# A block's down projection by seven products of half-size blocks in place of eight

## The chip, the cores and the metric

The kernel runs on one core of a Trainium2 chip. A core has five engines with instruction queues of their own, which run side by side and wait for each other through semaphores: TensorE (PE in the profile; its weight loads, PEld, overlap its matmuls), VectorE (DVE), ScalarE (ACT), GpSimd (POOL) and SyncE (SP, which here only starts transfers). SBUF is the on-chip memory of 128 partitions, PSUM the accumulator memory that TensorE writes and that VectorE and ScalarE read. The metric is the device time of one execution in microseconds, as the median of several.

## What is computed

The reference is a gated cross-attention followed by a gated feed-forward layer, for 8 sequences ("blocks") of 256 tokens with 1024 features. The change is in the second half:

```python
def qlinear(x, w):                       # fake_quant: s = max|t| / 127, q = round(t / s) * s
    xq = fake_quant(x, axis=-1)          # one step s for each token
    wq = fake_quant(w, axis=1)           # one step s for each output feature
    return jnp.einsum('bsh,oh->bso', xq, wq)
gate = qlinear(x, w_gate)                # 1024 -> 2752
up = qlinear(x, w_up)
h = jax.nn.silu(gate) * up
return qlinear(h, w_down)                # 2752 -> 1024, the "down" product
```

The result is multiplied by `tanh(g_ffn)` and added to the layer's input, the residual. The kernel keeps the rounded values as whole numbers of at most 127 in bf16 and applies the steps after the products.

## The kernel before

**Stages.** Up to about 457 us the kernel multiplies the two attention weights, runs attention for seven blocks and prepares the feed-forward weights: the down weights end as whole numbers in `wd`, 22 chunks of 128 rows by 1024 columns. Then comes the head, in which the last block's attention lies between the first block's gate and up products; then seven rounds of one block each; then a tail.

**Gate and up, `gate_up`.** A block's 2752 hidden features are 22 chunks, taken as 11 pairs. For each pair TensorE makes 64 passes of 128x256 (`products`, L787, the last pair 48) into one PSUM bank of tag g and one of tag tr. Two banks of each tag exist, so TensorE can be at most two pairs ahead. VectorE multiplies the gate by the token steps (L797, reads ps_g), ScalarE applies silu (L799), VectorE multiplies by the up value (L812, reads ps_tr), ScalarE takes absolute values (L818), and VectorE folds them into a running maximum (`fold`, L829, two SBUF inputs). The last pair has one half chunk, for which L812 reads ps_g as well.

**A round, for b = 1 to 7.** It runs the gate and up products of block b and then the down product of block b-1, while block b is being rounded. `block_max` (L845, L849) and `block_scales` (L857 to L865) turn the maximum into a row of inverse steps, `ib`. `quantised` multiplies each pair by `ib` on VectorE (L876, two SBUF inputs) and rounds it, on VectorE in one instruction (L878) or on ScalarE in two (L880, L881), into `hq`, bf16 of 128 x 2 x 256.

**The down product.** A block's output is two token halves t by two column halves of 512. `down_pair` (L890) makes, for each of the 11 pairs, two passes of 128x512 for each of these four quarters: 88 passes a block, into two banks each of the tags s and a. In the next round `down_end` finishes one quarter after each of the first gate and up pairs: VectorE reads the bank and multiplies by both steps (L907), GpSimd adds the residual (L910), which SyncE has loaded (L899), and GpSimd's queue starts the store (L911).

**The tail.** Block 7 has no products beside it: three quarters one after another, the fourth in two halves, the last addition on VectorE (L1040), the last store on SyncE.

**Order.** In the head all engines run in the order of the program. From the second block on, only TensorE's and VectorE's order is written by hand; the instructions of ScalarE, GpSimd and SyncE are placed by a scheduler.

## Time and profile before

| | us |
|---|---|
| median of 3 runs (932.33 to 933.81) | 932.4 |
| the profiled execution, whole | 931.42 |
| its span, first to last instruction | 929.6 |
| TensorE busy in the span | 923.5 (99%) |
| VectorE / ScalarE / GpSimd busy | 635.6 / 420.9 / 152.0 |
| the head, 457.0 to 506.7: VectorE, GpSimd busy | 31.9, 2.7 of 49.7 |
| the second block's gate and up, 506.7 to 544.7: VectorE, GpSimd busy | 29.2, 0.8 of 38.0 |
| a down product in the steady state, 601.7 to 621.1: VectorE, GpSimd busy | 11.7, 0.0 of 19.4 |
| gate and up in the steady state, 564.1 to 601.7: VectorE, GpSimd busy | 25.9, 7.6 of 37.6 |
| the tail, 906.0 to 929.6: TensorE, GpSimd busy | 19.3, 12.8 of 23.6 |

A line of the page or of its groups names a source line, an engine and an operation, then what it writes and reads with the shapes and the number of instructions, then the busy time in all, the mean of one in ns, and the idle time of the engine before it with what ended it. A line of the timeline has the start and the length in us first. The length of an instruction starts when it is issued, so it includes time in which it is held up; instructions of one engine overlap by about 0.08 us, so that a VectorE instruction of "0.69" follows the one before it after 0.61.

### The profile page before, as it was taken

How to read it: one execution, taken by the hardware profiler on the slowest of the kernel's cores; microseconds unless marked ns; L12 is line 12 of the kernel's file. 1: busy time of each engine (PE TensorE's matmuls, PEld its weight loads, DVE VectorE, ACT ScalarE, POOL GpSimd, SP SyncE). 2: the span in 40 equal slices, each digit the busy share in tenths (PEclk: the TensorE clock that was granted, in tenths of full speed). 3: DMA queues.
4: the chain of work that ended last, by engine and by line, in shares of the span. 5: the costliest groups of instructions: out<-in, count | busy, mean ns of one | idle time of the engine just before them, and what ended most of it. 6: DMA issues, size and time to landing. Idle time of an engine off the chain costs nothing.

```text
span 929.6 us, 14411 instructions
## 1 busy us (share of the span) xinstructions
PE 923.5 (99%) x5471; PEld 689.3 (74%) x5471; DVE 635.6 (68%) x1284; ACT 420.9 (45%) x720; POOL 152.0 (16%) x165
## 2 busy tenths in 40 slices
PE   9999999999999999999999999999999999999998
PEld 5444687878787878787878867858688685876854
DVE  5978845868686767776367778666576665757663
ACT  0123434454545445453547776444354544535440
POOL 0034211212121212132001003012030110302005
PEclk9999999999999999999999999999999999999999
DMA  9359977989888888997979985929669395782704
GB/s 334 119 156 316 297 185 235 230 248 241 247 246 252 238 252 227 247 242 241 235 265 320 321 295 200 344 79 385 204 244 336 84 377 172 280 299 94 303 1 159
DMA packets 139189, 221.96 MB, mean 239 GB/s; under 512 B 92056, under 2 KB 93360, under 8 KB 128880
## 3 DMA queue, kind: packets, MB, share of 16 engines
q1 hardware_dynamic: 129328, 196.12, 68.1%
q0 software_dynamic: 5040, 17.06, 4.7%
q10 hardware_dynamic: 4752, 7.87, 2.4%
q8 instruction: 43, 0.70, 0.3%
q14 instruction: 26, 0.21, 0.1%
HBM read 167.52 MB, written 32.26 MB: 215 GB/s over the span
## 4 chain that ended last, share of the span: by engine, by line
PE 94%; DMA 3%; DVE 1%; POOL 1%; SPq 0%; issue 0%; ACT 0%; POOLq 0%; DVEq 0%; ACTq 0%
PE ps_g L787 17%; PE ps_tr L787 16%; PE ps_g L548 15%; PE ps_s L548 9%; PE ps_a L890 7%; PE ps_s L890 7%; PE ps_s L566 6%; PE ps_a L595 6%; PE ps_tr L445 3%; PE ps_s L342 2%; PE ps_a L342 2%; PE ps_tr L342 1%; PE ps_g L342 1%; DMA raw<-in_L_ffn_w_gate_dram 1%; DMA w_dram<-wt 1%; POOL o L910 1%
## 5 line engine op out<-in xcount | busy, mean ns | idle before, releaser
L787 PEld LDWEIGHTS <-wp 128*128 128x128 bf16 x2752 | 269.3, 98 | 33.0 <-issue 0.3
L787 PE MATMUL ps_g<-xqb,wp 128*128 128x256 bf16 x1408 | 168.1, 273 | 0.0
L787 PE MATMUL ps_tr<-xqb,wp 128*128 128x256 bf16 x1344 | 161.1, 273 | 0.0
L548 PE MATMUL ps_g<-xT,mt 128*128 128x256 f32 x640 | 144.6, 379 | 0.2 <-ACT xT L468 0.2
L548 PEld LDWEIGHTS ps_g<-xT,mt 128*128 128x128 f32 x640 | 120.3, 190 | 19.1 <-issue 3.3
L890 PEld LDWEIGHTS <-hq 128*128 128x128 bf16 x726 | 71.1, 98 | 76.5
L799 ACT ACTIVATE g<-g,swg 128x256 f32<-128x256 f32 (+1 forms) x176 | 80.3, 499 | 59.4 <-DVE g L797 59.4
L812 DVE SCALAR_TENSOR_TENSOR h<-ps_tr,swu,g 128x256 f32<-128x256 f32 x168 | 74.0, 480 | 48.3 <-PE ps_tr L787 34.1
L220 POOL TENSOR_SCALAR raw<-raw,inv 128x1024 f32<-128x1024 f32 (+1 forms) x44 | 56.2, 1276 | 249.1 <-DVE inv L122 144.0
L910 POOL TENSOR_TENSOR o<-o,xr 128x512 f32<-128x512 f32 x31 | 39.2, 1265 | 309.5 <-DVE o L907 287.5
L797 DVE TENSOR_TENSOR g<-ps_g,sx 128x512 f32<-128x512 f32 x88 | 60.7, 690 | 40.0 <-PE ps_g L787 36.9
L548 PE MATMUL ps_s<-xT,mt 128*128 128x256 f32 x384 | 86.9, 379 | 0.0
L818 ACT ACTIVATE g<-h 128x512 f32<-128x512 f32 (+2 forms) x88 | 52.0, 591 | 72.8 <-DVE h L812 72.0
L890 PE MATMUL ps_a<-wd,hq 128*128 128x512 bf16 (+1 forms) x352 | 84.0, 366 | 0.0
L890 PE MATMUL ps_s<-wd,hq 128*128 128x512 bf16 x330 | 84.0, 379 | 0.0
L257 ACT ACTIVATE rq<-raw,nmagic 128x1024 bf16<-128x1024 f32 (+1 forms) x44 | 50.6, 1150 | 62.1 <-POOL raw L220 51.4
L548 PEld LDWEIGHTS ps_s<-xT,mt 128*128 128x128 f32 x384 | 71.2, 190 | 8.7
L876 DVE TENSOR_TENSOR h<-h,ib 128x512 f32<-128x512 f32 x88 | 57.3, 685 | 21.2 <-ACT ib L865 21.2
L829 DVE TENSOR_TENSOR acc<-acc,g 128x512 f32<-128x512 f32 (+2 forms) x88 | 61.6, 700 | 1.0
L566 PE MATMUL ps_s<-fT,H 128*128 128x256 f32 x256 | 58.9, 379 | 0.0
L595 PE MATMUL ps_a<-fn,pT 128*128 128x512 f32 x128 | 57.6, 592 | 0.0
L126 DVE TENSOR_REDUCE wam<-raw 128x1 f32<-128x1024 f32 (+1 forms) x44 | 53.3, 1212 | 5.2 <-DMA raw<-in_L_ffn_w_gate_dram 5.1
(169 smaller groups left out, 1001.5 us busy)
## 6 DMA issues: line engine op xcount, KB each, us to landing
wp<-w_dram SPq DMA_DIRECT2D x80, 1024.0 KB, 6.8
w_dram<-wt SPq DMA_DIRECT2D x43, 256.0 KB, 4.1
raw<-in_L_ffn_w_gate_dram SPq DMA_DIRECT2D x21, 512.0 KB, 5.2
raw<-in_L_ffn_w_up_dram SPq DMA_DIRECT2D x21, 512.0 KB, 4.7
fn<-in_ctx_dram SPq DMA_DIRECT2D x8, 1024.0 KB, 6.7
raw<-in_L_ffn_w_down_dram SPq DMA_DIRECT2D x16, 512.0 KB, 6.7
xr<-in_x_dram SPq DMA_DIRECT2D x16, 512.0 KB, 4.2
x_dram<-xr POOLq DMA_DIRECT2D x16, 512.0 KB, 4.6
```

The lines of the kernel that those rows point to most:

```text
L220: nc.gpsimd.tensor_scalar(raw[:n], raw[:n], inv, MAGIC, ALU.mult, ALU.add)
L342: nc.tensor.matmul(pm, lhsT=a[:, c, k * P : (k + 1) * P], rhs=b[:, c, :], start=start, stop=stop)
L548: nc.tensor.matmul(ph, lhsT=mt[:, k, j * P : (j + 1) * P], rhs=xT[:, k, :], start=(k == 0), stop=(k == KC - 1),)
L566: nc.tensor.matmul(ps[:, :L], lhsT=H[:, j, t * P : (t + 1) * P], rhs=fT[:, j, :], start=(j == 0), stop=(j == KC - 1),)
L595: nc.tensor.matmul(pas[h], lhsT=pT[:, l, :], rhs=f_tiles[b][:, l, halves[h]], start=(l == 0), stop=(l == NLT - 1),)
L787: nc.tensor.matmul(banks[slot // 2][:, slot % 2, :], lhsT=w[:, slot, k, :], rhs=block["xq"][:, k, :], start=(k == 0), stop=(k == KC - 1),)
L797: nc.vector.tensor_tensor(g, pg, block["sx"].to_broadcast((P, 2, TB)), ALU.mult)
L799: nc.scalar.activation(g[:n, i, :], g[:n, i, :], AF.Silu, scale=swg[:n, c : c + 1])
L812: nc.vector.scalar_tensor_tensor(h[:n, i, :], src, swu[:n, c : c + 1], g[:n, i, :], ALU.mult, ALU.mult)
L829: nc.vector.tensor_tensor(acc[:n, i, :], acc[:n, i, :], g[:n, i, :], ALU.max)
L876: nc.vector.tensor_tensor(h, h, ib.to_broadcast((P, 2, TB)), ALU.mult)
L890: nc.tensor.matmul(pds[t, half][:, cols], lhsT=hq[p][:, i, t * P : (t + 1) * P], rhs=wd[:, c, half * HB + cols.start : half * HB + cols.stop],
```

## The change

The down product of a block is a product of two 2x2 block matrices for each pair of chunks: even and odd chunk by two token halves, even and odd chunk by two column halves. The new kernel makes seven products in place of eight (`down_product`, m = 1 to 7), of sums and differences of the quarters. Sums of two whole numbers of at most 127 are exact in bf16.

- **Weights, once.** `weight_sums(p)` makes for each of the 11 pairs a difference of 128x1024 and a sum of 128x512 on VectorE, and a sum of 128x1024 on GpSimd, which overwrites parts of `wd`. They are in the head: pairs 0 to 2 between the two softmax halves, 3 to 6 ahead of the first gate and up pair, 7 to 10 after its pairs 3, 7, 8 and 9.
- **Hidden values, for each block.** `hidden_sums` makes 640 columns of sums for each pair in three instructions (256, 128, 256), on GpSimd during the gate and up products, in the tail on VectorE.
- **Outputs.** m3 and m4 are copied out of PSUM by ScalarE (`evicted`), then eight additions or subtractions on VectorE (`combined_down`) put the four quarters together. `down_end` scales a quarter by the token steps on ScalarE, and multiplies by the column steps and adds the residual on GpSimd. The residual's load moves from SyncE's to GpSimd's queue.
- **Order.** `block_max` comes after 15 passes of the down product (before: 32), `block_scales` after 27 (before: 48). Eight pairs are rounded during the down product and the last three during the next gate and up products.
- **First and last.** In the second block's gate and up products, and for block 7, four of the 11 multiplications by `ib` go to GpSimd. In the tail a share of the last two quarters is prepared ahead (`tail_share`, one on VectorE, one on GpSimd) and `tail_end` adds the last product to it.

```diff
-    def down_pair(pds, hq, p, keys, cols=slice(0, HB)):
-        for t, half in keys:
-            for i, c, n in parts_of(p):
-                nc.tensor.matmul(
-                    pds[t, half][:, cols], lhsT=hq[p][:, i, t * P : (t + 1) * P],
...
+    def weight_sums(p):
+        even, odd = wd[:, 2 * p, :], wd[:, 2 * p + 1, :]
+        nc.vector.tensor_tensor(wdiff[:, p, :], odd, even, ALU.subtract)
+        nc.vector.tensor_tensor(wsum[:, p, :], even[:, :HB], odd[:, HB:], ALU.add)
+        o = 2 * p * D + HB
+        nc.gpsimd.tensor_tensor(
+            wd_flat[:, o : o + D].rearrange("p (i d) -> p i d", i=2),
+            wd[:, 2 * p : 2 * p + 2, :HB], wd[:, 2 * p : 2 * p + 2, HB:], ALU.add,
+        )
+    def hidden_sums(gs, p, hq, parts=(0, 1, 2), engine=nc.gpsimd):
...
+            engine.tensor_tensor(g[:, 0:2, :], v[:, 0], v[:, 1], ALU.add)
+            engine.tensor_tensor(g[:, 2, :], v[:, 0, 0], v[:, 1, 1], ALU.add)
+            engine.tensor_tensor(g[:, 3:5, :], v[:, :, 1], v[:, :, 0], ALU.subtract)
+    def down_product(m, hq, gs, tag, cols=slice(0, HB), pairs=range(NPR), pm=None):
...
+                1: lambda: (gs[p][:, 2, :], wsum[:, p, lo]),
+                2: lambda: (gs[p][:, 1, :], even[:, lo]),
+                3: lambda: (hq[p][:, 0, :P], wdiff[:, p, hi]),
+                4: lambda: (hq[p][:, 1, P:], wdiff[:, p, lo]),
+                5: lambda: (gs[p][:, 0, :], odd[:, hi]),
+                6: lambda: (gs[p][:, 3, :], even[:, hi]),
+                7: lambda: (gs[p][:, 4, :], odd[:, lo]),
+    def down_end(b, t, half, c, sh, xr=None, queue=nc.gpsimd):
...
+        nc.scalar.activation(c, c, AF.Identity, scale=sh[:, t : t + 1])
+        nc.gpsimd.tensor_tensor(c, c, swd_bc[:, cols], ALU.mult)
+        nc.gpsimd.tensor_tensor(c, c, xr, ALU.add)
+        queue.dma_start(out=out[b, t * P : (t + 1) * P, cols], in_=c)
...
     for p in range(2, NPR):
-        hq.append(quantised(first["h"][p - 2], ib, p - 2, nc.scalar))
+        if p < 9:
+            hq[p - 2] = quantised(first["h"][p - 2], ib, nc.scalar)
...
+        if 2 < p < 7:
+            stepped(first["h"][p + 4], ib, nc.gpsimd)
+        if p > 6:
+            hq[p] = rounded(first["h"][p])
...
+            hidden_sums(gs, q, hq[q])
         gate_up(second, p, banks if p == 2 else None)
...
+        m3 = down_product(3, hq, gs, "s")
+        c3 = evicted(m3, "c3")
+        m4 = down_product(4, hq, gs, "a", pairs=range(4))
+        am = block_max(block, "g")
+        down_product(4, hq, gs, "a", pairs=range(4, NPR), pm=m4)
+        c4 = evicted(m4, "c4")
+        m2 = down_product(2, hq, gs, "s", pairs=range(5))
+        next_sh, ib = block_scales(b, am, "tr")
...
+        quantise(0, 1)
+        c21 = combined_down(sum_tile("c21"), m2, c4)
+        m5 = down_product(5, hq, gs, "a")
+        quantise(2, 3)
+        c12 = combined_down(sum_tile("c12"), m5, c3, ALU.subtract)
+        combined_down(c3, m2, c3)
+        combined_down(c4, c4, m5, ALU.subtract)
+        m1 = down_product(1, hq, gs, "s")
+        quantise(4)
...
+    for end, xr in zip(ends, xrs + [xr_tail[b - 1, 1, 1], xr_tail[b - 1, 0, 0]]):
+        down_end(*end, xr)
+    for p in range(NPR):
+        hidden_sums(gs, p, hq[p], (0,), nc.vector)
...
+    down_end(b, 1, 0, b21, sh, xr_tail[b, 1, 0], nc.sync)
...
+    down_end(b, 0, 1, b12, sh, xr_tail[b, 0, 1], nc.sync)
...
+    tail_share(1, 1, b3, sh, xr_tail[b, 1, 1], nc.vector)
+    tail_share(0, 0, b4, sh, xr_tail[b, 0, 0], nc.gpsimd)
...
+    for i in range(2):
         cols = slice(i * HB // 2, (i + 1) * HB // 2)
...
+        m7 = down_product(7, hq, gs, "s", cols)
+        tail_end(0, 0, m7, nsh, b4, cols)
```

## The prediction

> **What bounds the kernel now.** I read the page's busy table and its chain of waits first, then the groups, then the timeline of four places: a down product, a fold beside GpSimd, the head, the end.

> ```profile
> PE 923.5 (99%) x5471; PEld 689.3 (74%) x5471; DVE 635.6 (68%) x1284; ACT 420.9 (45%) x720; POOL 152.0 (16%) x165
> ...
> PE 94%; DMA 3%; DVE 1%; POOL 1%; SPq 0%; issue 0%; ACT 0%; POOLq 0%; DVEq 0%; ACTq 0%
> ```

> TensorE works throughout at the full granted clock (the page's PEclk row is 9 in all slices), and the list of TensorE's waits holds under 2 us. So a pass removed is time gained, as long as nothing else begins to hold TensorE. GpSimd is at 16%: the change fills it. The timeline of TensorE in a steady down product gives the price of a pass:

> ```profile
> 557.25 1.03 PE L890 MATMUL ps_s<-wd,hq 128*128 128x512 bf16 x4
> 558.11 1.03 PE L890 MATMUL ps_a<-wd,hq 128*128 128x512 bf16 x4
> ```

> Four passes start every 0.863 us: 0.216 us each (the "379 ns" of the groups is the length of one, mostly overlapped). The second thing to see is what VectorE and GpSimd do to each other, with and without company:

> ```profile
> 687.00 1.26 POOL L910 TENSOR_TENSOR o<-o,xr 128x512 f32<-128x512 f32 x1 [1.38 <-DVE o L907]
> 687.05 0.69 DVE L797 TENSOR_TENSOR g<-ps_g,sx 128x512 f32<-128x512 f32 x1
> 687.66 1.15 DVE L829 TENSOR_TENSOR acc<-acc,g 128x512 f32<-128x512 f32 x1
> ...
> 694.65 0.68 DVE L829 TENSOR_TENSOR acc<-acc,g 128x512 f32<-128x512 f32 x1
> ```
> ```profile
> 76.99 0.69 DVE L347 TENSOR_TENSOR A<-A,A 128x512 f32<-128x512 f32 x1
> 77.16 2.03 POOL L220 TENSOR_SCALAR raw<-raw,inv 128x1024 f32<-128x1024 f32 x1 [1.49 <-DVE inv L122]
> 77.59 0.68 DVE L347 TENSOR_TENSOR B<-B,B 128x512 f32<-128x512 f32 x1
> ...
> 103.75 1.12 POOL L220 TENSOR_SCALAR raw<-raw,inv 128x1024 f32<-128x1024 f32 x1 [1.95 <-DVE inv L122]
> ```

> The fold has two SBUF inputs and takes 1.15 instead of 0.68 beside GpSimd: it ends 0.55 after GpSimd's 688.26. L797, with one input in PSUM, is not touched. The other way, GpSimd's 1.12 became 2.03 behind two VectorE instructions back to back: it got in only after both.

> [...] Read alone, the first row could be a surcharge of 0.47 for each meeting. [...]

> **Prices.** VectorE, start to start: 0.61 for 512 f32 elements (L876, two in 1.29), about 1.0 ns an element and 0.1 fixed. No bf16 instruction with two SBUF inputs is in the trace. [...] GpSimd: 1.265 for 512 with two inputs (L910); its one-input rows, 1111 ns at 1024 and 843 at 704, show 0.25 fixed. So about 2.3 for 1024 and 1.9 for a pair's 256, 128 and 256; with 0.1 fixed (its smallest memset) 2.4 and 1.75. bf16 on GpSimd is not shown either. A store or load issued there costs 0.56, and 0.3 more between sum and store.

> **Part 1, the passes.** 77 for 88, eleven fewer: 2.37 us a block. Seven rounds: **-16.6**. Block 7 is counted in part 5.

> **Part 2, the head.** VectorE gets 11 x 0.95, GpSimd 11 x 2.3. VectorE is idle ahead of 458.4, but the sums stand behind the first softmax scale. Six instructions back to back, 459.3 to 462.2; GpSimd then takes its first sum to 464.7; eight more VectorE instructions end at 468.5. The first gate (L797) stood at 463.8: 4.7 late. ScalarE, in program order, turns the second probabilities late behind the first |h|, and the second attention product starts at 473.3 instead of 472.5. By pair 7, L812 ends at about 505.3 instead of 500.8. From there a pair costs VectorE: sums 0.95, start of GpSimd's sum 0.1, its 2.3 (the next L797 runs inside it), fold 0.6, L812 0.8 = 4.75, against TensorE's 3.49. Three such pairs: pair 10's L812 ends at 519.7. It reads the half chunk from a g bank that TensorE needs for the next group but one, which began at 510.2: **+9.5**. Bounds: +3 if the exclusion doesn't bind, +12 with 1.1 for 1024. Ahead of the end of the head GpSimd also holds the residual's stores behind seven sums (x2 from 470.1 to about 483.5); landing 4.6 later, 488.1, it is just in time for ScalarE's y0 at 489.

> **Part 3, the first hidden sums.** GpSimd starts when `ib` is there (518.2 before): four multiplications 5.1, 11 x 1.9 = 20.9, and it stands aside for 9 folds, 7 multiplications and 4 roundings of VectorE, 11.0. That is 37.0 after `ib`; m2's last pair is due at 544.7 + 7.3, that is 33.8 after it: **+3.2** (0 to 7).

> **Part 4, a steady round**, 54.6 us long, T from the first down pass. GpSimd: 8 x 1.265 for the outputs, 20.9, 8 transfers 4.5, gaps 1.2, memset 0.3: 37.0. Its first output is ready at T+9.95 (m2 ends at 7.7, two multiplications and a rounding, the sum, ScalarE's scale). It stands aside for 9 multiplications, 3 roundings, 10 folds: 12.5. So it is done at 59.4, T+4.8 of the next down product; m2's last pair is due at T+7.3. Spare 2.5: **0**, and a loss if a pair costs over 2.1. Everything else fits. `block_max` comes 3.24 after the first pass, and the folds end at 2.95 (604.66 against 601.71). The second transposes come 2.81 behind it, and ScalarE's input takes 2.36 (608.62 to 610.98). VectorE: 37.6 busy, plus 8 x 0.61, minus 4 x 0.74 for L907, is 39.5 of 54.6. ScalarE: 26.8, plus two copies, four scalings, one rounding more (about 5.4), is 32 of 54.6. SyncE loses four loads; its weight loads don't move. Two banks of each tag let VectorE be about 4 us late in gate and up, and waits for GpSimd of some 0.5 a fold stay inside that.

> **Part 5, the last down product and the tail.** From T+6.9 GpSimd has 18 instructions in a fixed order: 4 multiplications, 8 for block 6, 6 for block 7. The last of them is the share of the last quarter, for which `tail_end` waits. 18 x 1.265 = 22.8. VectorE's excluded work in the same stretch: 7 multiplications 4.2, 7 roundings 2.5, 33 hidden sums 6.1, the other share 1.2: 14.0. One at a time they need 36.8, so the share can't be there before T+43.7, that is 26.6 after the tail's start (T+17.05); walked in order, with the hidden sums back to back ahead of GpSimd, 28.9. I take 27.5. Then addition, product, addition 1.3, and 3.2 to the end as now (926.44 to 929.6): 32.0. TensorE is done long before, at 16.8. Before, 906.05 to 929.6 is 23.55: **+8.5**. The bounds: without exclusion GpSimd ends at 16, TensorE is last again and the tail is 2.4 shorter; +10 by the walk, +13 with one bf16 element a cycle.

> **Sum** on the profiled execution's 931.4: -16.6 + 9.5 + 3.2 + 0 + 8.5 = +4.6, so 936.0. The median before is 1.0 above that execution; I predict **936.5**.

> **Rivals.** (a) *The exclusion is only paid in the tail*, where both engines are full; in the head and the second block VectorE's spare time takes it: -16.6 + 3 + 8.5 = -5.1, **926**. For it: VectorE was busy 31.9 of 49.7 in the head; against it: part of that idle time is the wait for silu, which stays. (b) **Faster on one mechanism: meetings cost a surcharge of 0.47, or GpSimd slips in between VectorE's instructions.** Then a pair in the head costs VectorE 3.4, under 3.49, GpSimd has room in parts 3 to 5, and TensorE stays the bound: -16.6 - 2.4 + 3 = -16, **915.5**. The exclusion costs 20.6 us in the forecast; the kernel breaks even where it costs 16. Against it: the 2.03 row. (c) *GpSimd becomes the bound of each round*: bf16 sums at 2.5 a pair. The spare 2.5 turns into 4.1 late, six times, and part 3 grows by 6.6: 936.5 + 24.6 + 6.6 = **968**. That the passes are not saved is no rival: the built order shows 77 a block.

> **Chances.** Forecast 0.48, (a) 0.19, (b) 0.17, (c) 0.16. The forecast's own range is 930 to 943. To hold 8 of 10 the range reaches to (a), into the upper half of (b) and to the milder sizes of (c): 917 to 948. A difference of 0.2%, 1.9 us, is about what these measurements can tell. The forecast is slower but for 0.04 same and 0.03 faster; (a) is faster but for 0.03 same; (b) faster, (c) slower: faster 0.36, same 0.07, slower 0.57.

> **What will show it.** Right: 16.6 us fewer passes; weight sums on GpSimd of about 2.3, with folds of 2 us or more beside them; TensorE's waits for VectorE's L812 in the last head pairs, and for GpSimd's hidden sums once; a tail of some 32 us whose chain ends in GpSimd, with TensorE idle for its last 15. Wrong: folds of at most 1.2 beside GpSimd, TensorE busy to within 5 us of the end, or hidden sums far from 1.9 a pair.

## The result, and the profile after

The changed kernel takes **948.92 us** (median of six runs, 948.08 to 951.0), the kernel before 932.38 in the same comparison: ratio 1.0178, interval [1.0164, 1.0192]. It is slower, as forecast, but by 16.5 us, four times the forecast 4.1, and just above the range. The profiled execution took 951.0 us with a span of 949.2; spans are compared below, and 949.2 against 929.6 is 19.6 us more. About 3 us of these are the choice of execution: the profiled one is the slowest of the six, and the one before was faster than its median.

From the page of the kernel after come the busy table, the clock row and the chain of waits:

```profile
PE 914.1 (96%) x5372; PEld 681.6 (72%) x5372; DVE 742.5 (78%) x1367; ACT 447.9 (47%) x768; POOL 408.6 (43%) x469
...
PEclk9999999999999999999979999999999999999998
...
PE 81%; DVE 8%; issue 3%; POOL 2%; ACT 2%; DMA 2%; POOLq 0%; DVEq 0%
```

TensorE works 9.4 us less and the span is 19.6 longer, so TensorE idles some 29 us more. VectorE's busy time grew by 107 us and GpSimd's by 257; both include time in which one is held by the other (a `wdiff` of 2.61 us for 0.69, at 460.96; a hidden sum of 0.87 for 0.42, at 550.28). A clock row that was 9 throughout now has a dip in the middle and one at the end. The longest of TensorE's waits (line, what it waited for: total, times, longest):

```profile
PE ps_tr L787 <- DVE h L812: 9.9, 4, 8.3
PE ps_g L845 <- DVE acc L839: 2.9, 1, 2.9
PE ps_g L940 <- ACT hq L883: 2.8, 2, 2.2
PE ps_g L787 <- DVE h L812: 2.6, 1, 2.6
PE ps_s L940 <- DVE c L954: 2.0, 1, 2.0
```

Cut at the first pass of each stage, the two traces differ like this (us of span, stage by stage; positive is slower):

| stage | forecast | measured |
|---|---|---|
| up to the second block's second gate pair (the head) | +9.5 | +18.3 |
| rest of that block's gates, first down product (3.2 - 2.4) | +0.8 | +3.9 |
| five steady rounds | -11.9 | -11.9 |
| block 6's down product | -2.4 | -0.2 |
| last down product and tail | +8.5 | +9.5 |
| sum | +4.6 | +19.6 |

About 1 us of the head's figure is there before the first weight sum: the first softmax maximum (L574) was at 458.40 before and is at 459.24.

**The head, read from the timeline** (start, length, engine, line; in brackets the idle time before and what ended it). Three lines of the kernel before, then those of the kernel after:

```profile
458.40 0.43 DVE L574 TENSOR_REDUCE nm<-ps_s 128x1 f32<-128x256 f32 x1 [8.11 <-PE ps_s L566]
...
463.82 0.69 DVE L797 TENSOR_TENSOR g<-ps_g,sx 128x512 f32<-128x512 f32 x1 [1.10 <-PE ps_g L787]
...
470.77 1.91 PE L787 MATMUL ps_tr<-xqb,wp 128*128 128x256 bf16 x16
```

```profile
460.02 0.69 DVE L904 TENSOR_TENSOR wdiff<-wd 128x1024 bf16<-128x1024 bf16 x1
...
460.63 0.42 DVE L905 TENSOR_TENSOR wsum<-wd 128x512 bf16<-128x512 bf16 x1
460.86 2.17 POOL L907 TENSOR_TENSOR wd<-wd 128x1024 bf16<-128x1024 bf16 x1 [8.12 <-issue]
460.96 2.61 DVE L904 TENSOR_TENSOR wdiff<-wd 128x1024 bf16<-128x1024 bf16 x1
...
463.83 2.60 DVE L904 TENSOR_TENSOR wdiff<-wd 128x1024 bf16<-128x1024 bf16 x1
...
467.39 1.38 DVE L576 SCALAR_TENSOR_TENSOR nm<-cq,nm 128x1 f32<-128x1 f32 x1
...
478.21 0.68 DVE L797 TENSOR_TENSOR g<-ps_g,sx 128x512 f32<-128x512 f32 x1
...
480.40 3.57 PE L787 MATMUL ps_tr<-xqb,wp 128*128 128x256 bf16 x16 [8.31 <-DVE h L812]
```

The first `wdiff` is free and takes 0.69. GpSimd's sum is issued 0.15 after that, at 460.86, while `wsum` runs to 461.05. The second `wdiff` is issued 0.10 after GpSimd's sum and takes 2.61: it ends 0.54 after the whole of GpSimd's sum. So a pair costs 2.86 us (460.96 to 463.83), seven pairs and the two maxima hold VectorE for 18 us, and the gate product of pair 0, which VectorE took up at 463.82 before, starts at 478.21. TensorE has filled its banks by 472 and idles 8.31. Its next sixteen passes then take 3.57, where the same group took 1.91 before (470.77). The stretches of this time say why; after the length come busy PE, PEld, DVE, ACT and POOL (with counts), then the granted clock, DMA share and GB/s:

```profile
480.00:484.00 4.00, 3.60 (x17) 2.61 (x17) 2.63 (x6) 2.88 (x5) 0.84 (x2) 0.50 0.21 38
...
516.00:520.00 4.00, 3.51 (x34) 2.98 (x32) 4.00 (x7) 2.22 (x5) 2.74 (x2) 1.00 0.74 284
```

The granted clock is 0.50 in the first stretch after the wait: the idle time costs again, about 2.4 us in the two groups after it (3.57 for 1.91, then 4.38 for the 3.60 of before). In the lower row, where pairs 8 to 10 are on, VectorE is busy 4.00 of 4.00 us and TensorE is not; folds take 2.01 there behind a weight sum. Together: 8.3 idle, 2.4 of clock, 5.4 from pair 8 on, where VectorE is full, and some 2 of drift and small waits.

**The tail:**

```profile
921.12 1.59 PE L940 MATMUL ps_g<-wdiff,hq 128*128 128x512 bf16 x5 [2.19 <-ACT hq L883]
...
922.50 4.10 PE L940 MATMUL ps_tr<-wdiff,hq 128*128 128x512 bf16 x11
...
940.97 1.26 POOL L1152 TENSOR_TENSOR h<-h 128x512 f32<-128x512 f32 x1
942.26 0.43 DVE L1160 TENSOR_TENSOR h<-h 128x256 f32<-128x256 f32 x1 [2.10 <-POOL h L1152]
```

The first product waits for roundings of the hidden values, and the next eleven passes take 4.10 instead of 2.54. The end waits for GpSimd's share, as forecast: it is there 26.1 us after the tail's start (916.16).

### The profile page after: what moved, and what is told of

It reads as the page before. It is cut to its first block, busy times and chain, and to the rows that moved or that the text cites. A ratio compares the mean times of both kernels' runs of the same rounds, so it can differ in the third digit from the quotient of the medians.

```text
span 949.2 us, 14725 instructions
## 1 busy us (share of the span) xinstructions
PE 914.1 (96%) x5372; PEld 681.6 (72%) x5372; DVE 742.5 (78%) x1367; ACT 447.9 (47%) x768; POOL 408.6 (43%) x469
## 4 chain that ended last, share of the span: by engine, by line
PE 81%; DVE 8%; issue 3%; POOL 2%; ACT 2%; DMA 2%; POOLq 0%; DVEq 0%
PE ps_g L548 14%; PE ps_g L787 12%; PE ps_tr L787 12%; PE ps_s L548 8%; PE ps_s L940 6%; PE ps_s L566 5%; PE ps_a L595 5%; PE ps_a L940 5%; PE ps_s L342 4%; PE ps_tr L445 3%; PE ps_a L342 3%; DVE h L812 2%; DVE wdiff L904 2%; PE ps_tr L342 1%; PE ps_g L342 1%
## 5 line engine op out<-in xcount | busy, mean ns | idle before, releaser
L787 PEld LDWEIGHTS <-wp 128*128 128x128 bf16 x2752 | 270.7, 98 | 49.7 <-issue 15.8
L787 PE MATMUL ps_tr<-xqb,wp 128*128 128x256 bf16 x1344 | 163.9, 275 | 10.1 <-DVE h L812 9.9
L220 POOL TENSOR_SCALAR raw<-raw,inv 128x1024 f32<-128x1024 f32 (+1 forms) x44 | 56.1, 1276 | 247.5 <-DVE inv L122 163.1
L829 DVE TENSOR_TENSOR acc<-acc,g 128x512 f32<-128x512 f32 (+2 forms) x88 | 95.0, 1081 | 2.4
L799 ACT ACTIVATE g<-g,swg 128x256 f32<-128x256 f32 (+1 forms) x176 | 79.8, 497 | 29.2 <-DVE g L797 29.1
L812 DVE SCALAR_TENSOR_TENSOR h<-ps_tr,swu,g 128x256 f32<-128x256 f32 x168 | 73.8, 477 | 22.2 <-ACT g L799 14.3
L940 PEld LDWEIGHTS <-gs 128*128 128x128 bf16 x451 | 44.2, 98 | 51.8 <-issue 2.6
L875 DVE TENSOR_TENSOR h<-h,ib 128x512 f32<-128x512 f32 x80 | 67.2, 854 | 16.4 <-ACT ib L865 16.4
L968 POOL TENSOR_TENSOR c<-c,swd_bc 128x512 f32<-128x512 f32 x28 | 37.2, 1329 | 87.5 <-issue 76.8
L797 DVE TENSOR_TENSOR g<-ps_g,sx 128x512 f32<-128x512 f32 x88 | 60.0, 681 | 13.6 <-PE ps_g L787 13.6
L923 POOL TENSOR_TENSOR gs<-hq 128x256 bf16<-128x256 bf16 x77 | 68.9, 895 | 0.0
L919 POOL TENSOR_TENSOR gs<-hq 128x256 bf16<-128x256 bf16 x77 | 58.2, 755 | 2.3 <-ACT hq L883 2.0
L882 ACT ACTIVATE h<-h,magic 128x512 f32<-128x512 f32 x53 | 38.2, 721 | 40.9 <-DVE h L875 40.4
```

What stands on the lines that cost most here:

```text
L787: nc.tensor.matmul(banks[slot // 2][:, slot % 2, :], lhsT=w[:, slot, k, :], rhs=block["xq"][:, k, :], start=(k == 0), stop=(k == KC - 1),)
L797: nc.vector.tensor_tensor(g, pg, block["sx"].to_broadcast((P, 2, TB)), ALU.mult)
L799: nc.scalar.activation(g[:n, i, :], g[:n, i, :], AF.Silu, scale=swg[:n, c : c + 1])
L812: nc.vector.scalar_tensor_tensor(h[:n, i, :], src, swu[:n, c : c + 1], g[:n, i, :], ALU.mult, ALU.mult)
L829: nc.vector.tensor_tensor(acc[:n, i, :], acc[:n, i, :], g[:n, i, :], ALU.max)
L875: engine.tensor_tensor(h, h, ib.to_broadcast((P, 2, TB)), ALU.mult)
```

## The experiments

Theory A after the result: the head's excess is the way in which GpSimd and VectorE take turns in the weight sums, the rest the forecast's own terms. Rivals: the sums are too much for VectorE wherever they are made; or only program order lets GpSimd in. "The head" below is the time from the first softmax maximum (L574) to the first gate product (L797): 5.4 us before, 19.0 after, 10.1 in the forecast. The ratios are to the kernel before, timed beside each. Every kernel below starts from the changed one.

| label | us | ratio [95%] | head, us |
|---|---|---|---|
| `sums_all_vector` | 936.99 | 1.0044 [1.003, 1.0059] | 12.3 |
| `pool_sums_after` | 949.8 | 1.0179 [1.0159, 1.0199] | as after |
| `pool_sums_in_quarters` | 938.62 | 1.0074 [1.0045, 1.0104] | 13.7 |
| `filler_in_the_wait` | 947.51 | 1.0158 [1.0127, 1.0189] | as after |
| `pool_sums_held_back` | 944.46 | 1.0137 [1.0122, 1.0153] | 8.1 |
| `held_back_in_quarters` | 946.43 | 1.0157 [1.0136, 1.0177] | 8.1 |
| `last_steps_on_vector` | 948.78 | 1.0183 [1.0168, 1.0198] | as after |
| `last_share_first` | 949.62 | 1.02 [1.0183, 1.0217] | as after |
| `tail_reordered` | 936.17 | 1.0049 [1.0028, 1.007] | 12.3 |
| `weights_in_the_gaps` | 937.82 | 1.0068 [1.0053, 1.0083] | 3.7 |
| `no_pool_in_round_0` | 945.39 | 1.0142 [1.0119, 1.0166] | 5.4 |
| `round_0_and_end_ordered` | 942.35 | 1.0114 [1.0097, 1.013] | 5.4 |
| `tail_by_eight` | 948.95 | 1.0175 [1.0155, 1.0195] | as after |
| `head_on_vector_tail_by_eight` | 934.86 | 1.0034 [1.0023, 1.0045] | 7.3 |
| `tail_banks_apart` | 933.5 | 1.0012 [1.0003, 1.0021] | 7.3 |

### GpSimd out of the weight sums

```diff
-        nc.gpsimd.tensor_tensor(
+        nc.vector.tensor_tensor(
             wd_flat[:, o : o + D].rearrange("p (i d) -> p i d", i=2),
```

> The third sum of each pair (L907) moves from GpSimd to VectorE, where it should take about 0.61 us as wdiff does, so that no GpSimd sum stands between two VectorE sums. Theory (the two engines exclude each other while both read SBUF, and GpSimd is let in after each wsum): a pair costs VectorE about 1.63 us instead of 2.86, the first gate multiplication starts near 472 us instead of 478.2, TensorE's wait for the first hidden h shrinks from 8.3 to 2-3 us, kernel about 939 us. Rival (VectorE simply has too much work, no exclusion): 0.61 us more for each of the first seven pairs, gate at about 482, kernel about 953 us.

936.99: 12 us come back. From its timeline, a pair in full:

```profile
458.49 0.68 DVE L904 TENSOR_TENSOR wdiff<-wd 128x1024 bf16<-128x1024 bf16 x1
459.09 0.42 DVE L905 TENSOR_TENSOR wsum<-wd 128x512 bf16<-128x512 bf16 x1
459.42 0.68 DVE L907 TENSOR_TENSOR wd<-wd 128x1024 bf16<-128x1024 bf16 x1
```

VectorE makes all three sums of a pair in 1.54 us, less than it loses by handing one of them to GpSimd (2.86). TensorE's wait for the first hidden value falls from 8.3 to 2.0. From the first maximum to the first down product it takes 93.9 us instead of 105.4 (86.3 before).

### Called later, held back, cut in four

The first seven of GpSimd's sums are called after the first gate product:

```diff
     gate_up(first, 0)
+    for p in range(7):
+        weight_folds(p)
```

> The first seven GpSimd sums are called after the first block's first hidden product instead of each beside its VectorE sums; nothing else moves. This is what the prediction assumed to happen by itself: VectorE alone first, then GpSimd. Theory: wdiff takes 0.6 us everywhere, first gate multiplication at 468-468.5 us, TensorE's wait before the second pair's up products under 0.5 us, no lowered clock there; kernel about 938 us (10-11 us less than the changed kernel; pairs 8 to 10 still cost their 6 us). Rival (the VectorE sums are slow by themselves, or wait for the transfers of the down weights): wdiff stays at 2.6 us and the time at 949 us.

No change at all, and the expectation failed for a plain reason: GpSimd had nothing else in its queue, so each sum still began as its `wdiff` ended, and five `wdiff`s take 2.60 or 2.61 as in the changed kernel. A later place in the program held back nothing on this empty queue. The next kernel puts the same loop behind the first residual's store, which GpSimd issues and which waits for attention:

```diff
     nc.gpsimd.dma_start(out=x2_dram[last], in_=xr[0])
+    for p in range(7):
+        weight_folds(p)
```

> The run pool_sums_after moved the GpSimd sums in the program but behind nothing that holds GpSimd up, so each still started when its wdiff was done. Here the first seven stand behind the transfer of the first residual (L995), whose data come from VectorE only after the first gate product: VectorE must do its 14 sums without GpSimd. Theory (exclusion, GpSimd let in after every second VectorE sum): every wdiff 0.6 us (pitch), first gate multiplication 9 us after the first softmax maximum instead of 19.0, TensorE's wait before the second pair's up products 0 to 0.5 us instead of 8.3, from first softmax maximum to first down product about 95 us instead of 105.4; kernel 938 to 939 us. Rival (the work itself on VectorE is too much, wherever GpSimd is): no more than 3 us gained, 946 us or more.

Now VectorE's fourteen sums run at their own 0.69 and 0.42, and the head is 8.1 us, even shorter than forecast. But of the 10.9 us gained in the head only 4.5 reach the end; the rest is given back at once, as the timeline shows:

```profile
472.39 14.60 POOL L909 TENSOR_TENSOR wd<-wd 128x1024 bf16<-128x1024 bf16 x7
...
479.54 8.00 DVE L829 TENSOR_TENSOR acc<-acc,g 128x512 f32<-128x512 f32 x1
```

VectorE's fold arrives in GpSimd's fourth sum and waits until the seventh ends at 486.99, not for the end of the fourth (about 480.7). Here the turn is not handed over between instructions. The other way of making the turns smaller, each sum in four pieces of 256 columns:

```diff
+        for i in range(2):
+            for lo in (0, HB // 2):
...
+                nc.gpsimd.tensor_tensor(
+                    wd_flat[:, o + lo : o + hi], wd[:, 2 * p + i, lo:hi],
+                    wd[:, 2 * p + i, HB + lo : HB + hi], ALU.add,
+                )
```

> Each GpSimd sum of 1024 columns becomes four of 256, about 0.6-0.7 us each. If the two engines take turns instruction by instruction (theory), each VectorE sum waits for one short instruction only: wdiff about 1.2 us, wsum about 1.0, first gate near 476.5, kernel 946-947 us. If GpSimd, once in, keeps its turn until its queue is empty, wdiff stays at 2.6 us or longer, kernel 949-950 us. If VectorE's issue order alone counts (no exclusion), nothing changes: 949 us.

10 us come back, more than expected:

```profile
459.44 21.48 POOL L910 TENSOR_TENSOR wd<-wd 128x256 bf16<-128x256 bf16 x28 [8.13 <-DVE wdiff L904]
459.54 1.16 DVE L904 TENSOR_TENSOR wdiff<-wd 128x1024 bf16<-128x1024 bf16 x1
```

Here the two engines do take turns: a `wdiff` takes 1.16, waiting some 0.5 for one piece, and a pair costs 1.9. Both edits together ask which of the two it is:

> As pool_sums_held_back, with each GpSimd sum of 1024 columns in four of 256. There one VectorE instruction (the first fold L829) took 8.00 us, until the last of the seven GpSimd sums was done. Theory A (GpSimd keeps its turn while its next instruction is ready at once): the same 28 quarters run on in 14.6 us and the fold again takes 7 to 8 us, kernel 943-945 us. Theory B (turns change at the end of every instruction, and the long ones were let through for another reason): the fold takes at most 1.3 us, the two waits of TensorE of 2.5 and 2.2 us behind it shrink, kernel about 939 us.

```profile
480.73 10.94 DVE L829 TENSOR_TENSOR acc<-acc,g 128x512 f32<-128x512 f32 x1
```

The fold waits again until the last of the 28 pieces, which run from 473.58 to 491.13. Why pieces alternate with the bf16 sums and not with this f32 fold stays open. The type alone is not the reason. In `pool_sums_in_quarters` itself a later fold stood 2.85 us through four pieces, but in the second block of the changed kernel a fold was let in after one hidden sum of GpSimd, and the next one was held instead:

```profile
549.69 1.18 DVE L829 TENSOR_TENSOR acc<-acc,g 128x512 f32<-128x512 f32 x1
...
550.28 0.87 POOL L921 TENSOR_TENSOR gs<-hq 128x128 bf16<-128x128 bf16 x1
```

What else differs, such as a queue of VectorE without a gap, was not tried apart.

### The lowered clock

64 passes of no use go into a bank that is written again anyway, ahead of the group that waits, so that TensorE isn't idle:

```diff
+        if block is first and p == 1:
+            for _ in range(64):
+                nc.tensor.matmul(banks[0][:, 0, :], ..., start=True, stop=True)
```

> 64 passes more than the kernel needs, written to the pair's own gate bank just before its real gate products, fill TensorE's wait before the second pair's up products (64 x 0.109 = 7.0 us of 8.3). Theory (TensorE is slow after it has waited): the up products after it take 1.75 us instead of 3.36, the attention group 3.5 instead of 4.2, kernel 2 to 2.5 us faster than the changed one, about 946.5 us. Rival (the slow groups have another cause, or the clock falls for the work itself): 949 us or more.

```profile
480.14 1.91 PE L793 MATMUL ps_tr<-xqb,wp 128*128 128x256 bf16 x16 [1.64 <-DVE h L818]
```

The group behind the wait takes 1.91 again instead of 3.57: it was the idle time that lowered the clock, which reads 1.00 from 480 to 484 instead of 0.50. At the first down product this kernel is 3.0 us ahead of the changed one (102.4 us behind the first maximum instead of 105.4); half of it goes again at the wait for the folds, behind which the clock is lowered for 6.8 us instead of 3.4. In the total it is 1.4 us, and the intervals of the two kernels overlap: the mechanism is shown by the row, the gain is not by the times.

### The tail, with seven products

Three edits moved work away from GpSimd at the end, or changed its order.

```diff
                 if final and q > 6:
+                    stepped(block["h"][q], ib)
                     next_hq.append(rounded(block["h"][q]))
...
-                stepped(block["h"][q], ib, nc.gpsimd)
```

> Only the last round is changed: the four multiplications of h by ib that GpSimd does there (L875, 6.5 us for four) go to VectorE (0.61 us each, alone). Theory (in the last round VectorE waits on GpSimd more than it is helped): L875 and L880 on VectorE fall from about 1.4 and 1.3 us to 0.7 and 0.4, TensorE's waits of 2.0 us before m7 and 4 us in m3 of the tail go down to under 1 us in all, kernel 3 to 4.5 us faster than the changed one, about 945. Rival (the tail is set by GpSimd's last shares alone): the last round gains nothing that reaches the end, 948.5 to 949. Rival (VectorE lacks the time): 2.4 us of multiplication more, 950 to 951.

```diff
-    down_end(b, 0, 1, b12, sh, xr_tail[b, 0, 1], nc.sync)
...
     tail_share(0, 0, b4, sh, xr_tail[b, 0, 0], nc.gpsimd)
+    down_end(b, 0, 1, b12, sh, xr_tail[b, 0, 1], nc.sync)
```

> Only GpSimd's order at the end is changed: the share of the last block (tail_share of b4, L1151 and L1152) stands before the end of b12 instead of behind it. Theory (the last 5 us hang on GpSimd's chain b21, b12, b4 of 3 us each, and b4's is the only one that VectorE's last two blocks wait for): VectorE's last sum comes 2 to 3 us earlier, b12's transfer becomes the last one, 1.5 to 2.5 us gained, about 946.8 us. Rival (the end is set by transfers and the closing of the kernel): 948.5 to 949.

```diff
+    m3 = down_product(3, hq, gs, "g", pairs=range(7))
+    m4 = down_product(4, hq, gs, "tr", pairs=range(7))
+    down_product(3, hq, gs, "g", pairs=range(7, NPR), pm=m3)
+    down_product(4, hq, gs, "tr", pairs=range(7, NPR), pm=m4)
```

> On sums_all_vector (936.99 us), only the end is changed: m3 and m4 of the last block first over pairs 0 to 6, then over the last four pairs, whose hq come late; and the share of b4 stands before the end of b12 on GpSimd. Theory (part of the tail is TensorE waiting for the last hq, 1.8 to 4 us with half the clock after it, and VectorE waiting for GpSimd's last share, 2.1 us): the tail from its first pass to the end falls from 31.4 to 28 us, kernel about 933.5 us. Rival (the tail is bound by VectorE's own work from the last hq on): less than 1 us gained.

None gained. With the last four multiplications on VectorE, the 2.0 us wait in block 6's down product went (16.8 us instead of 19.2), and came back as waits of 3.2 and 2.2 for the roundings in the tail: VectorE has no time there. The second says nothing of its theory: GpSimd's instructions are put in order by the scheduler, and their order did not change. The third (with all sums on VectorE, so to be held against 936.99, and with the move of the second) left the tail at 31.9, where it was 31.4. The changed kernel ends 7.0 us after GpSimd's last addition (942.23 and 949.2), and `sums_all_vector` too (926.82 and 933.8): with that, an edit gains there only as far as GpSimd ends earlier.

### The head by spreading, and the first round without GpSimd

`weights_in_the_gaps` has all sums on VectorE, four pairs ahead of the first maximum, one between the two, and the rest one instruction to a gate product, with the two tail edits above.

```diff
     scores(pss[0], 0, range(KC))
+    weight_step(12)
...
     gate_up(first, 3)
-    weight_sums(7)
+    weight_step()
```

> All three sums of weights on VectorE, four pairs before the first softmax maximum where VectorE waits 8.1 us for scores, one pair between the two softmax maxima, and the last six pairs one sum at a time after each gate product; with the two edits of the tail (multiplications of the last round on VectorE, share of b4 first). Theory: the head costs 1 to 2 us over the kernel before instead of 16 to 19, the last round and tail 4 over; with 16.6 saved in passes of which 2.4 in every round show: about 925 us, under the kernel before by 0.8%. Rival (the sums cost VectorE time that shows wherever they stand): no better than sums_all_vector less the tail's gain, 931-932.

The four pairs push the first maximum itself to 461.13, since the memory of `wdiff` is free only at 454.96. At 498 us the kernel was still only 1.04 behind the one before, and 5.5 more were lost from the second block's first pass to the first down product: VectorE had weight sums left there, beside GpSimd's hidden sums, and TensorE then waited 3.4 for the folds. `no_pool_in_round_0` therefore moved the first round's hidden sums and multiplications from GpSimd to VectorE as well, and part of the weight sums behind the first down product.

```diff
-            stepped(first["h"][p + 4], ib, nc.gpsimd)
+            stepped(first["h"][p + 4], ib)
...
+            hidden_sums(gs, q, hq[q], (0, 1), nc.vector)
```

> No GpSimd arithmetic at all until the second block's h are quantised: sums of weights on VectorE (two pairs before the first softmax maximum, one between the maxima, the others one or two instructions after each gate product, the last five in the first down product), the multiplications of h by ib and the sums of hidden blocks of round 0 on VectorE too; with the end of tail_reordered. Theory (in round 0 the exclusion costs VectorE more than the work it is spared: each two-input instruction beside GpSimd is 0.3 to 0.6 us longer, some 40 of them): VectorE's L829 and L875 fall to 0.6-0.7 us, from the first softmax maximum to the end of the first down product the kernel is within 3 us of the kernel before (105.75 us there), and the whole about 927 to 930 us, under the kernel before. Rival (VectorE's work is the limit in round 0, wherever it runs): 935 us or more.

VectorE's folds and multiplications all took 0.68, and up to 493 us the kernel was 0.2 behind the one before. By the gate pair at 522.57 it was 4.9 behind, by small waits. Then something else was late:

```profile
531.91 3.53 PE L787 MATMUL ps_g<-xqb,wp 128*128 128x256 bf16 x16 [5.69 <-DMA wp<-w_dram]
```

The transposing load of the next tokens (L764) was issued at 510.0, ahead of weights, and TensorE waited 5.7 for them, the sixteen passes after it taking 3.53 instead of 1.91; 4.7 more went to weight sums that GpSimd held up in the first down product. `round_0_and_end_ordered` puts SyncE in program order, these sums ahead, and GpSimd's end in an order by hand.

```diff
-        tc.manual_schedule(engines={mybir.EngineType.PE, mybir.EngineType.DVE})
+        tc.manual_schedule(engines={mybir.EngineType.PE, mybir.EngineType.DVE, mybir.EngineType.SP})
```

> As no_pool_in_round_0, with what its trace showed mended: the sync engine's transfers of the rounds in program order (there the transposing load of the next tokens went ahead of the weights and TensorE waited 5.7 us for wp), the last six in-place sums of wd ahead of the quantising in the first down product (there m6 waited 4.7 us for them, held up by GpSimd's ends of the output), two of them in VectorE's wait for ib, and GpSimd's order at the end by hand, share of b4 before the end of b12 (in last_share_first and tail_reordered GpSimd's order had stayed as it was). Theory: the two waits of 5.7 and 4.7 us and the lowered clock behind them go (12 to 14 us), VectorE's last wait of 2.1 us too: 929 to 932 us, about the kernel before or 0.3% under it. Rival (VectorE's own work in round 0 is the limit): those waits come back as waits for VectorE, 938 us or more.

Both waits went, and the first down product began only 3.2 us later than before. But that product took 23.4 us where its passes need 17.05, the gate and up products after it were 4.6 longer (VectorE behind), and the tail was 33.7. VectorE's work moved is VectorE's work due a stage later.

### The tail by eight products

The last block goes back to eight products of 11 passes, on the weights as the sums have left them. With E and O for the weight rows of a pair's two hidden chunks and 0 and 1 for the output halves, `wd` holds E0, E0 + E1, O0 + O1 and O1. For each half of the tokens x is the even chunks by E0 and y the odd ones by O1; the first output is the odd chunks by O0 + O1, plus x - y, and the second is the even chunks by E0 + E1, minus x - y.

```diff
+    terms = [(0, 0, bank("g")), (0, 1, bank("tr")), (1, 0, bank("s")), (1, 1, bank("a"))]
+    for pairs in (range(7), range(7, NPR)):
+        for t, i, pm in terms:
+            down_terms(pm, t, i, i, pairs, True, True)
```

> Only the last block's down product is changed: eight products of half-size blocks again, without sums of hidden blocks (the overwritten halves of wd are got round by x - y of two products, as even.hi = sum - even.lo), first over pairs 0 to 6 of four products (28 passes, 6.0 us), then over pairs 7 to 10, whose hq come last. Theory (the tail's 9.5 us over the kernel before are TensorE's waits for hq and for sums of hidden blocks, and the last chain of GpSimd's shares): the tail falls from 33.0 us to 88 x 0.2155 = 18.96 us of passes, at most 1 us of waits, 1.5 us of VectorE and 3.2 to 5.7 us of closing, 24.5 to 27 us; kernel 940 to 942.5 us. Rival (VectorE's quantising and the lowered clock set the tail, whatever the products): 946 us or more. If the closing is 5.7 us here too, its 2.5 us over the kernel before do not come from the end's work.

33.6 us for the tail, no gain: 3.2 of waits for the roundings, and one of the experiment's own, since the two halves of the last half-block share a bank. The same tail with all weight sums on VectorE (two pairs ahead of the first maximum) was expected to add the two gains:

> The tail of tail_by_eight on the head of sums_all_vector, with two pairs of sums before the first softmax maximum, one between the two, two behind and the last six pairs one by one after later gate products, and the sync engine's transfers in program order in the rounds. Theory (head and tail are separate losses that add up, five rounds keep their 2.37 us): from the first softmax maximum to the second down product 146 to 149 us (143.7 in the kernel before, 150.0 in sums_all_vector), five rounds at 54.6, the tail 24.5 to 27: 924 to 929 us, 0.4 to 0.9% under the kernel before. Rival (VectorE's work, moved, shows again in the first rounds as in round_0_and_end_ordered): 933 us or more.

With 934.86 it missed the total; the head is as hoped (91.0 us from the first maximum to the first down product), the tail is 33.7 with the same wait:

```profile
926.25 2.50 PE L1173 MATMUL ps_a<-wd,hq 128*128 128x256 bf16 x11 [3.67 <-DVE h L1160]
```

Then this wait was taken away, the second half of the last quarter going into another bank; VectorE was also relieved of one share (the lines are against the kernel just shown):

```diff
-        parts = 2 if (t, half) == (1, 1) else 1
...
+    last_pass(1, 1, "a", slice(0, HB // 2))
+    last_pass(1, 1, "g", slice(HB // 2, HB))
```

> As head_on_vector_tail_by_eight (934.86 us, tail of 33.7 us), but the two halves of the last half-block go into different banks, and VectorE ends the first half-block before it works on shares; one share of the second tile moves from VectorE to GpSimd. Theory (the tail's loss is TensorE's own wait of 3.67 us for the bank with half clock behind it, then VectorE's queue): the wait before the last half-pass goes, TensorE ends near 924.0 instead of 928.75 on the time axis of that profile; VectorE then sets the end: its chain from 916.7 is first end 1.45, the share 1.4 to 2, then ends of 1.45 + 1.45 + 0.9 + 0.9, so the last sum ends at 925.2 to 926.5 instead of 929.74, 3.2 to 4.5 us earlier: 930.4 to 931.7 us, tail 29.2 to 30.5. Rival (VectorE or GpSimd has no time and the wait comes up elsewhere, as in the earlier attempts on the tail): last sum no more than 1.5 us earlier, 933.4 us or more.

The tail fell to 28.2 us (903.44 to 931.6), better than the 29.2 to 30.5 expected, and the total only to 933.5, which is where the rival had it (933.4 or more). The 5.5 us are seen where they were sought, but the span is only 1.3 shorter (931.6 for 932.9). Of the 4.2 us between, 1.0 is there before the first maximum, and 1.7 and 1.5 come in two places where both kernels have the same program and the same waits to a tenth. One group of passes behind the same wait of 2.0, in `head_on_vector_tail_by_eight` and then in `tail_banks_apart`:

```profile
896.87 2.53 PE L940 MATMUL ps_s<-wd,gs 128*128 128x512 bf16 x11 [2.00 <-DVE c L954]
```

```profile
899.58 4.07 PE L940 MATMUL ps_s<-wd,gs 128*128 128x512 bf16 x11 [2.00 <-DVE c L954]
```

In the first execution the clock stayed at 1.00 there, in the second it fell (0.68 in the stretch 899 to 903), 1.5 us. Behind the 2.9 us wait for the folds it is the same, and costs 1.7. Two stretches of 3.41 us around that wait, first of `head_on_vector_tail_by_eight`, then of `tail_banks_apart`:

```profile
550.15:553.56 3.41, 1.63 (x8) 0.54 (x6) 3.29 (x6) 2.27 (x6) 3.27 (x6) 1.00 0.97 347
553.56:556.98 3.42, 2.31 (x12) 1.25 (x13) 2.14 (x8) 0.62 (x3) 1.49 (x3) 1.00 0.75 145
```
```profile
552.24:555.66 3.42, 0.57 (x3) 0.07 (x1) 3.16 (x6) 1.59 (x4) 3.28 (x6) 1.00 1.10 337
555.66:559.07 3.41, 3.36 (x9) 1.48 (x10) 1.22 (x6) 0.69 (x2) 0.43 (x1) 0.50 0.45 63
```

The wait lies across two stretches in the first, with 1.63 and 2.31 of matmuls, and within one in the second, with 0.57; how the stretches are cut is told at the end.

No changed kernel came out under the one before: the last is at 1.0012, within what counts as no difference.

## Why the forecast was wrong

Of the 15 us between forecast and measurement in the table, the head makes 8.8, the first round 3.1, block 6's down product 2.2 and the tail 1.0. By its own sum the forecast was 937.0 (936.0 and the 1.0 between median and profile) and not 936.5; that decides nothing.

**Part 1, the passes: right.** A steady round takes 54.6 us, 2.37 less than before, five times over.

**Part 2, the head: the step that failed.** The forecast said: "Six instructions back to back, 459.3 to 462.2; GpSimd then takes its first sum to 464.7; eight more VectorE instructions end at 468.5." It took from the row of 2.03 that GpSimd gets in only when VectorE pauses. The runs showed the reverse. GpSimd got in beside the `wsum` of each pair, with no pause of VectorE. VectorE waited out five of the first seven sums in full, with a `wdiff` of 2.60 instead of 0.69 and 2.86 for the pair instead of 0.95, and a sixth in part. What the forecast calls the exclusion, that VectorE with two SBUF inputs and GpSimd wait out the whole of each other's instruction, agrees with its two rows (1.15 for 0.68, 2.03 for 1.12), and the head shows it: 2.61 against 0.69 for one `wdiff`, which ended 0.54 after GpSimd's sum. The order was another matter. GpSimd's sum was issued at 460.86, the second `wdiff` at 460.96, and the `wdiff` waited. The forecast let one row (2.03) speak for the order, and there it was the other way round: GpSimd's instruction was issued at 77.16, VectorE's second at 77.59, and the second went first. `pool_sums_held_back` is the proof from the other side: with GpSimd kept away, the head was 8.1 us long, under the 10.1 of the forecast. No one order holds in all the runs, as the last section shows. The second term missed was the clock, 2.4 us in the head: the trace before, at 1.00 throughout, had no idle time to show it. The term for pairs 7 to 10, folds behind a 2.3 us sum, was right in kind (2.01); a pair cost 4.26 there for 4.75.

**Rival (b)** had the event, "GpSimd slips in between VectorE's instructions", and the wrong price for it. Slipping in was thought to cost a surcharge of 0.47; in the head it cost 1.91 (a `wdiff` of 2.60 for 0.69, beside a sum of 2.23). The break-even of 16 us stood in the text; all that the change added came to 36.2 (19.6 and the 16.6 saved), where the forecast had 21.2.

**Part 3, the first hidden sums: near in size, wrong in cause.** The first round lost 6.3 beside its 2.4 saved, against 3.2 forecast. TensorE's list has no wait for GpSimd's hidden sums. The 6.3 are the 2.9 of wait for the folds and two lowered stretches of 3.4 us at 529.7 and 570.7, up to 1.7 each. VectorE was late, not GpSimd: its folds took 0.94 to 1.18 beside GpSimd's instructions instead of 0.68, and the block began behind the head's last wait.

**Part 4: right.** GpSimd needed 2.2 us a pair for the hidden sums, held time included, instead of 1.9. That is over the 2.1 from which the forecast expected a loss, and the round still did not wait.

**Part 5: right in size, 33.0 for 32.0, in part by luck.** GpSimd's share came at 26.1 for 27.5. The closing, from VectorE's last sum to the end, took 5.7 instead of 3.2. So two errors nearly cancel: the end hangs on GpSimd itself, 7.0 us after its last addition, and not on VectorE's last sums (last section). TensorE was not done at 16.8 but at 22.3, by its waits for roundings (2.19 the longest) and the halved clock (eleven passes in 4.10 for 2.54). Of what was named as "right" signs, the folds of 2 us and the end in GpSimd's share came true; "TensorE idle for its last 15" was 10.7.

**Block 6's down product** was counted as a saving of 2.37 without a term of its own and saved 0.2: a wait of 2.0 for VectorE's combination is new there.

The price of the bf16 sums, 0.95 us for a pair's two on VectorE and 6.1 for the 33 hidden sums of the tail, is shown by no row of the kernel before. It was right: in the trace after, a `wdiff` of 1024 elements takes 0.61 and a `wsum` of 512 0.33, start to start (460.02, 460.63, 460.96), 0.94 together. With no GpSimd arithmetic beside them, eleven hidden sums of 256 took 2.30 (929.45) and eleven of 128 1.56 (927.96), which makes 6.2 for the 33; the first eleven, beside GpSimd, took 5.43 (922.61). The bound of "one bf16 element a cycle" is shown by no run either.

## What to carry to other kernels

Before giving work to GpSimd beside a VectorE that reads two operands from SBUF, compare VectorE's own price with GpSimd's duration, because here VectorE paid the second: a sum of 0.61 us on VectorE itself, given to GpSimd, made it wait 1.9. A stage in which TensorE never waits gives no hint of what a wait costs: behind waits of 2.0, 2.2 and 8.3 us here, a group of passes took 1.5 to 1.7 us longer in some executions (4.07 for 2.53, 4.10 for 2.54, 3.57 for 1.91). Let GpSimd end early: what it did last was followed by 7.0 us here, a last sum of VectorE by 3.2 where GpSimd had ended early. Where two engines can both be next, one row does not tell who is; cost both orders.

## What the runs showed of the hardware

```profile
932.85 1.59 POOL L1194 TENSOR_TENSOR h<-h 128x512 f32<-128x512 f32 x1
```

In `tail_banks_apart` both meet, 7.0 us after the one and 3.1 after the other. What the 7.0 us are spent on no run shows.
